# Rows left unnormalised between three attention layers, the mean taken out of the weights, and five groups of graphs in work instead of four

## The chip, the cores and the metric

The kernel runs on one core of one Trainium2 chip, in float32 throughout. The metric is device time in microseconds (us) of one execution. Before the change it takes 2701.81 us, the median of three runs (2700.86 to 2701.89). The profiled execution has a span of 2698.8 us and was itself timed at 2700.63 us; its granted TensorE clock averages 0.998. Engines are named as in the profile: PE (matmuls), DVE (VectorE), ACT (ScalarE), POOL (GpSimd), SP (the queue that issues DMAs).

## The reference

There are 128 graphs of 128 nodes, each node a row of 256 numbers `x`, and each graph has an adjacency matrix. Four layers follow one another, each adding its result to its input and normalising every row:

```python
x = layernorm(x + ggnn(x, adj, ...))          # three GRU steps, each: h@W, A^T@(...), GRU cell
x = layernorm(x + gat(x, adj, W1, a1))        # three attention layers of the form
x = layernorm(x + gat(x, adj, W2, a2))        #   Wh = x @ W.T;  e = leaky(Wh@a1 + (Wh@a2).T)
x = layernorm(x + gat(x, adj, W3, a3))        #   p = softmax(where(adj == 0, -inf, e));  p @ Wh
layernorm(x) = (x - mean(x)) / sqrt(var(x) + 1e-5)     # per row, no gain and no offset
```

In the second attention layer a node without neighbours gets zero in place of the attention result.

## The kernel before

**Groups.** Four graphs make a group (`G = 4`), so there are 32 groups. A group's rows lie as 128 partitions by 4 x 256. Each group goes through `gru` (three GRU steps) and then `gat` (three attention layers).

**GRU.** A step transposes or reads the hidden state, multiplies by the adjacency (L504), and forms the gates with a Strassen scheme: seven products of 128-row blocks per pass, two passes per step (L451, 8064 of the 14536 matmul records). DVE adds partial products (L456), ACT applies tanh (L530, L559), DVE blends (L546, L566, L569), and PE transposes the new state back (L585). The last step adds the state to `x` (L588), and the row normalisation at the end of `gru` gives `x1`.

**Attention.** Each layer of `gat` does, for its four graphs: two dot products per row against weight vectors (L611, eight DVE instructions with accumulated sums, written to `f`); PE spreads one of them over columns (L620); DVE adds the mask and takes the row maximum (L625); ACT applies the leaky slope (L629) and the exponential with its row sum (L646); PE transposes the result (L653), which is copied out of PSUM to `pT` (L655); PE multiplies the layer's input by it (L669), the product is copied out (L672), and PE multiplies by the layer's weights `gwT` (L680). DVE scales each row by the reciprocal of the softmax sum, `rden`, adds the layer's input and accumulates the row sum `total` (L686). Then comes `layernorm`.

**`layernorm` (L375 to L409).** After the GRU it uses DVE's batch statistics (L382, L384). After an attention layer it takes the mean from `total` (DVE, L391), the squares from four ACT instructions (L394), the variance plus epsilon on POOL (L397), the power -1/2 on POOL (L401), the shift on DVE (L403), and writes the normalised rows with four ACT instructions (L407). The next layer's L611 reads those rows.

**Order of the work.** Nothing is scheduled at run time. `Plan` (L48 to L195) takes the operations with assumed costs and walks a clock: an operation becomes ready when its inputs are done, and the ready one of lowest priority number starts on a free engine if buffers are free. Each engine then executes its own operations strictly in that fixed order, with waits on the others. An operation may name several engines (`EVICT` is ACT at 490 or DVE at 600), and the walk chooses. For PE, an operation whose input comes from another engine counts as ready only after that engine's `LATENCY` and a further `MARGIN` of 500 ns (L56, L117). Buffers come from pools of fixed size (L224): `gru` is a token that limits how many groups are in their GRU part (4), `k2` and `k4` hold half-size and full-size tiles, `v` small vectors. `own` (L226) reserves some of a pool for the oldest group. `stage` (L696) gives the first 28 groups their number as priority and lets the last four (`LAST = 4`) advance step by step together.

**Weights.** `score_weights` (L346) loads a layer's weights in both layouts while group 0 runs and forms the vectors `wa` that L611 uses; `gwT` is the layout that L680 reads.

Of the kernel before, what the change touches and what calls it, by code (L numbers as in the profile page):

```python
# [11 lines left out]
ALU = mybir.AluOpType  # L12
# [35 lines left out]
class Plan:  # L48
# [6 lines left out]

    MARGIN = 500  # L56

# [141 lines left out]
def adj_resnorm_kernel(  # L199
# [23 lines left out]

    pools = {"gru": 4, "xs": 2, "adj": 2, "am": 5, "k2": 26, "k4": 19, "fx": 2, "f": 3, "mv": 4, "st": 6, "v": 16,  # L224
             "gate": 5, "bank": 3}
    own = ({"k2": 8, "k4": 5, "gate": 2, "v": 5, "fx": 0, "st": 0}, {"k2": 4, "k4": 2, "v": 5, "fx": 0, "st": 0})  # L226
    floats = {"gru": 0, "k4": 1024, "xs": 1024, "fx": 256, "f": 8, "mv": 8, "st": 6, "v": 4}
    tags = {t: (n, floats.get(t, 512)) for t, n in pools.items()}
# [117 lines left out]
    def score_weights(l, prio):  # L346

        gatw, b_ = Buf("k2", KC, D), bank()
        load(gatw, gat_w[:, l], prio, start=30000)
        load(here(T(gwT)[:, l]), gat_wT[:, l], prio, start=30000)  # L350

        def fn(e):
            for h in range(2):
                for k in range(KC):
                    nc.tensor.matmul(T(b_)[:, h * D:(h + 1) * D], ga[:, l, k, h:h + 1].to_broadcast([P, P]),
                                     T(gatw)[:, k, :], start=(k == 0), stop=(k == KC - 1))
        plan.op({"PE": 4 * 432}, fn, reads=[gatw], writes=[b_], prio=prio)
        plan.op(EVICT, lambda e: copy(e, T(wa)[:, l, :, :].rearrange("p h d -> p (h d)"), T(b_)),
                reads=[b_], writes=[(wa, l)], prio=prio)
# [14 lines left out]

    def layernorm(y, total, dst, prio):  # L375

        rstd, ve, shift = Buf("v", G), Buf("v", G), Buf("v", G)
        if total is None:
            mv = Buf("mv", G, 2)
            for b in range(G):  # L380
                st = Buf("st", 6)
                plan.op({"DVE": 400}, lambda e, b=b, st=st: nc.vector.bn_stats(T(st), T(y)[:, b, :]),  # L382
                        reads=[(y, b)], writes=[st], prio=prio)
                plan.op({"DVE": 95}, lambda e, b=b, st=st: nc.vector.bn_aggr(T(mv)[:, b, :], T(st)),  # L384
                        reads=[st], writes=[(mv, b)], prio=prio)
            plan.op({"POOL": 229}, lambda e: nc.gpsimd.tensor_scalar(T(ve), T(mv)[:, :, 1], EPS, None, op0=ALU.add),
                    reads=[(mv, b) for b in range(G)], writes=[ve], prio=prio)
            less, keys = (lambda: T(mv)[:, :, 0]), [(mv, b) for b in range(G)]
        else:
            mean, ss = Buf("v", G), Buf("v", G)  # L390
            plan.op({"DVE": 100}, lambda e: nc.vector.tensor_scalar(T(mean), T(total), -1.0 / D, None, op0=ALU.mult),  # L391
                    reads=[(total, b) for b in range(G)], writes=[mean], prio=prio)
            for b in range(G):
                plan.op({"ACT": 490}, lambda e, b=b: nc.scalar.activation(  # L394
                    T(dst)[:, b, :], T(y)[:, b, :], AF.Square, bias=T(mean)[:, b:b + 1], accum_out=T(ss)[:, b:b + 1]),
                    reads=[(y, b), mean], writes=[(dst, b), (ss, b)], prio=prio)
            plan.op({"POOL": 229}, lambda e: nc.gpsimd.tensor_scalar(  # L397
                T(ve), T(ss), 1.0 / D, EPS, op0=ALU.mult, op1=ALU.add),
                reads=[(ss, b) for b in range(G)], writes=[ve], prio=prio)
            less, keys = (lambda: T(mean)), [mean]  # L400
        plan.op({"POOL": 1035}, lambda e: nc.gpsimd.tensor_tensor(T(rstd), T(ve), neghalf, ALU.pow),  # L401
                reads=[ve], writes=[rstd], prio=prio)
        plan.op({"DVE": 100}, lambda e: nc.vector.scalar_tensor_tensor(  # L403
            T(shift), less(), -1.0 if total is None else 1.0, T(rstd), op0=ALU.mult, op1=ALU.mult),
            reads=keys + [rstd], writes=[shift], prio=prio)
        for b in range(G):
            plan.op({"ACT": 500}, lambda e, b=b: nc.scalar.activation(  # L407
                T(dst)[:, b, :], T(y)[:, b, :], AF.Identity, bias=T(shift)[:, b:b + 1], scale=T(rstd)[:, b:b + 1]),
                reads=[(y, b), shift, rstd], writes=[(dst, b)], prio=prio)  # L409

    def sums(ms, prio):
# [65 lines left out]
    def gru(g, stage):  # L477
# [119 lines left out]
        x1 = Buf("k4", G, D)  # L597
        layernorm(y, None, x1, prio)
        return x1, am

    def gat(g, xc, no, stage):

        for l in range(3):
            prio = stage(g, STEPS + l)
# [3 lines left out]
            for h in (1, 0):  # L608
                for b in range(G):
                    fx = Buf("fx", D)  # L610
                    plan.op({"DVE": 345}, lambda e, b=b, h=h, l=l, f=f, fx=fx, xc=xc: nc.vector.scalar_tensor_tensor(  # L611
                        T(fx), T(xc)[:, b, :], 1.0, T(wa)[:, l, h, :], op0=ALU.mult, op1=ALU.mult,
                        accum_out=T(f)[:, b, h:h + 1]), reads=[(xc, b), (wa, l)], writes=[fx, (f, 2 * b + h)], prio=prio, port=BOTH)
            e_, pT, y = Buf("k2", G, P), Buf("k2", G, P), Buf("k4", G, D)
            top, nmax, den, rden, total = Buf("v", G), Buf("v", G), Buf("v", G), Buf("v", G), Buf("v", G)
            b_ = bank()
# [34 lines left out]
            def fn(e, b_=b_, e_=e_):  # L651
                for b in range(G):
                    nc.tensor.transpose(T(b_)[:, b * P:(b + 1) * P], T(e_)[:, b, :], ident)  # L653
            plan.op({"PE": 440}, fn, reads=[(e_, b) for b in range(G)], writes=[b_], prio=prio)
            plan.op(EVICT, lambda e, b_=b_, pT=pT: copy(e, T(pT).rearrange("p b j -> p (b j)"), T(b_)),  # L655
                    reads=[b_], writes=[pT], prio=prio)
            plan.op({"DVE": 100}, lambda e, rden=rden, den=den: nc.vector.reciprocal(T(rden), T(den)),
                    reads=[(den, b) for b in range(G)], writes=[rden], prio=prio)
            if l == 1:
                plan.op({"DVE": 100}, lambda e, rden=rden, some=some: nc.vector.tensor_mul(T(rden), T(rden), T(some)),  # L660
                        reads=[rden, some], writes=[rden], prio=prio)

            aT = []
# [10 lines left out]
            for b0 in range(0, G, 2):  # L674
# [9 lines left out]
                for b in (b0, b0 + 1):  # L684
                    plan.op({"DVE": 410}, lambda e, b_=b_, b=b, b0=b0, y=y, rden=rden, xc=xc, total=total:
                            nc.vector.scalar_tensor_tensor(  # L686
                                T(y)[:, b, :], T(b_)[:, (b - b0) * D:(b - b0 + 1) * D], T(rden)[:, b:b + 1],
                                T(xc)[:, b, :], op0=ALU.mult, op1=ALU.add, accum_out=T(total)[:, b:b + 1]),
                            reads=[b_, rden, (xc, b)], writes=[(y, b), (total, b)], prio=prio)
            xn = Buf("k4", G, D)  # L690
            layernorm(y, total, xn, prio)
            xc = xn
        plan.op({"SP": 60}, lambda e: nc.sync.dma_start(out[g * G:(g + 1) * G].rearrange("b n d -> n b d"), T(xc)),
# [56 lines left out]
```

## Time and profile before

| | before |
|---|---|
| timed runs, median (lowest to highest) | 2701.81 us (2700.86 to 2701.89) |
| span of the profiled execution | 2698.8 us |
| busy: PE / DVE / ACT / POOL | 2655.6 / 2019.6 / 1758.2 / 603.7 us |
| instructions: PE / DVE / ACT / POOL | 14536 / 6195 / 4633 / 749 |
| L611 dot products, DVE, x768 | 290.3 us |
| L407 normalised rows, ACT, x512 | 263.6 us |
| L394 squares, ACT, x384 | 190.2 us |
| L686 scale and add, DVE, x384 | 169.9 us |
| L403 shift and L391 mean, DVE | 35.0 and 25.4 us |
| HBM traffic | 62.7 MB, 23 GB/s |

The page gives the busy time of each engine, its share of the span, and the same in 40 equal slices as tenths. A group's row gives the line, engine, tiles, shapes and count, then its total and mean duration, then the idle time of that engine ahead of it and what ended that idle time. A busy PE is not the same as a PE at its rate, since the ends of matmuls are modelled; the distance between starts in the timeline is the better measure. All DMA queues together use under a tenth of the DMA engines' time.

### The profile page before, as it was taken

Reading aid. Unit: us, or ns where it says so; the run is one execution under the profiler, and the core shown is the slowest. Engines: PE = TensorE matmul, PEld = TensorE weight load, DVE = VectorE, ACT = ScalarE, POOL = GpSimd, SP = SyncE. Lnnn points to the kernel's source line nnn. Section 1 sums busy time; section 2 is a strip of 40 time slices with the busy share of each in tenths; the row PEclk is TensorE's granted clock in tenths of the full one; section 3 lists DMA queues with packets and bytes.
Section 4 is the critical chain, followed back from the end, with each engine's and each line's share of the span. In section 5 each row is a group of like instructions: output and inputs, shape, how many; then the busy total and the mean of one; then the engine's idle time right before and its main releaser. Section 6 shows DMA issues by size and latency. Waiting matters only on the chain.

```text
span 2698.8 us, 42460 instructions
## 1 busy us (share of the span) xinstructions
PE 2655.6 (98%) x14536; PEld 2366.9 (88%) x14536; DVE 2019.6 (75%) x6195; ACT 1758.2 (65%) x4633; POOL 603.7 (22%) x749
## 2 busy tenths in 40 slices
PE   8999999999999999999999999999999999999997
PEld 7888889898888888888888888988988988888875
DVE  4676777787777787778777777877778776786796
ACT  4565667666667576666666676666666676765478
POOL 1123222222121221222221221211222211322111
PEclk9999999999999999999999999999999999999999
DMA  3100000000000000001010000000000100000000
GB/s 106 32 13 28 28 13 24 28 29 20 16 21 20 28 28 28 28 1 36 21 36 13 20 24 21 28 28 20 17 28 21 36 21 1 24 9 22 19 1 32
DMA packets 70105, 65.39 MB, mean 24 GB/s; under 512 B 2688, under 2 KB 68224, under 8 KB 69888
## 3 DMA queue, kind: packets, MB, share of 16 engines
q1 hardware_dynamic: 69456, 62.66, 7.7%
q8 instruction: 114, 1.87, 0.3%
q14 instruction: 103, 0.84, 0.1%
q10 hardware_dynamic: 432, 0.01, 0.0%
HBM read 45.89 MB, written 16.78 MB: 23 GB/s over the span
## 4 chain that ended last, share of the span: by engine, by line
PE 90%; DVE 6%; ACT 2%; issue 1%; DMA 0%; POOL 0%; POOLq 0%; ACTq 0%; SPq 0%; DVEq 0%
PE gate L451 61%; PE bank L680 10%; PE bank L504 6%; PE bank L669 6%; PE bank L585 3%; PE bank L620 1%; PE bank L653 1%; DVE fx L611 1%; PE bank L369 1%; PE bank L338 1%; DVE k L686 1%; ACT k L407 1%; DVE k L456 1%; DVE k L289 1%; ACT k L394 0%
## 5 line engine op out<-in xcount | busy, mean ns | idle before, releaser
L451 PE MATMUL gate<-k,whs 128*128 128x256 f32 x4032 | 1201.6, 380 | 3.0 <-DVE k L456 1.4
L451 PE MATMUL gate<-k,wcs 128*128 128x256 f32 x4032 | 1199.2, 379 | 0.0
L451 PEld LDWEIGHTS gate<-k,wcs 128*128 128x128 f32 x4032 | 766.1, 190 | 104.0
L451 PEld LDWEIGHTS gate<-k,whs 128*128 128x128 f32 x4032 | 728.5, 190 | 85.3 <-DVE k L456 2.7
L456 DVE TENSOR_TENSOR k<-gate,k 128x512 f32<-128x512 f32 x576 | 390.4, 686 | 242.3 <-PE gate L451 200.2
L287 ACT COPY k<-bank 128x512 f32<-128x512 f32 (+1 forms) x456 | 262.2, 583 | 207.4 <-PE bank L669 60.9
L680 PE MATMUL bank<-gwT,k 128*128 128x256 f32 x1536 | 350.4, 380 | 3.3 <-ACT k L287 1.5
L680 PEld LDWEIGHTS bank<-gwT,k 128*128 128x128 f32 x1536 | 289.7, 190 | 46.0 <-DVE k L289 4.3
L611 DVE SCALAR_TENSOR_TENSOR fx<-k,wa 128x256 f32<-128x256 f32 x768 | 290.3, 436 | 40.3 <-ACT k L407 38.2
L421 POOL TENSOR_TENSOR k<-k,k 128x256 f32<-128x256 f32 x288 | 236.0, 838 | 372.8 <-DVE k L569 103.6
L394 ACT ACTIVATE k<-k,v 128x256 f32<-128x256 f32 x384 | 190.2, 497 | 185.6 <-DVE v L391 185.1
L407 ACT ACTIVATE k<-k,v,v 128x256 f32<-128x256 f32 x512 | 263.6, 591 | 55.9 <-DVE v L403 53.9
L530 ACT ACTIVATE k<-k,brz 128x512 f32<-128x512 f32 (+1 forms) x384 | 226.9, 620 | 93.2 <-DVE k L456 93.1
L686 DVE SCALAR_TENSOR_TENSOR k<-bank,v,k 128x256 f32<-128x256 f32 x384 | 169.9, 480 | 147.0 <-PE bank L680 145.8
L512 ACT COPY k<-gate 128x512 f32<-128x512 f32 x288 | 164.6, 579 | 127.9 <-PE gate L451 127.0
L564 POOL TENSOR_TENSOR k<-k,k 128x512 f32<-128x512 f32 x82 | 108.5, 1324 | 418.0 <-ACT k L559 418.0
L669 PEld LDWEIGHTS bank<-k,k 128*128 128x128 f32 x1536 | 187.1, 193 | 14.6 <-ACT k L287 5.4
L669 PE MATMUL bank<-k,k 128*128 128x128 f32 x1536 | 189.8, 277 | 8.0 <-DVE k L289 4.0
L289 DVE COPY k<-bank 128x512 f32<-128x512 f32 x228 | 154.3, 684 | 56.2 <-PE bank L504 18.3
L559 ACT ACTIVATE k<-k,bi 128x512 f32<-128x512 f32 x192 | 136.8, 720 | 76.3 <-DVE k L556 59.2
L397 POOL TENSOR_SCALAR v<-v 128x4 f32<-128x4 f32 x96 | 21.1, 220 | 739.3 <-ACT k L394 733.3
L421 POOL TENSOR_TENSOR k<-k 128x256 f32<-128x256 f32 x117 | 100.2, 858 | 340.4 <-DVE k L569 118.2
(78 smaller groups left out, 3166.8 us busy)
## 6 DMA issues: line engine op xcount, KB each, us to landing
xs<-in_x_dram SPq DMA_DIRECT2D x32, 512.0 KB, 3.9
k<-in_x_dram SPq DMA_DIRECT2D x32, 512.0 KB, 3.9
out_dram<-k SPq DMA_DIRECT2D x32, 512.0 KB, 2.9
adj<-in_adj_dram SPq DMA_DIRECT2D x32, 256.0 KB, 2.8
k<-in_gnn_wT_dram SPq DMA_DIRECT2D x3, 256.0 KB, 4.8
k<-in_w_ihT_dram SPq DMA_DIRECT2D x2, 384.0 KB, 5.7
k<-in_w_hhT_dram SPq DMA_DIRECT2D x2, 384.0 KB, 5.7
k<-in_gat_w_dram SPq DMA_DIRECT2D x3, 256.0 KB, 5.1
```

The lines of the kernel that those rows point to most:

```text
L287: nc.scalar.copy(dst, src)
L289: nc.vector.tensor_copy(dst, src)
L394: plan.op({"ACT": 490}, lambda e, b=b: nc.scalar.activation(T(dst)[:, b, :], T(y)[:, b, :], AF.Square, bias=T(mean)[:, b:b + 1], accum_out ...
L407: plan.op({"ACT": 500}, lambda e, b=b: nc.scalar.activation(T(dst)[:, b, :], T(y)[:, b, :], AF.Identity, bias=T(shift)[:, b:b + 1], scale= ...
L421: nc.vector if e == "DVE" else nc.gpsimd).tensor_tensor(T(t)[:, j, :], a(), b(), ALU.subtract),
L451: nc.tensor.matmul(T(dst)[:, j * H:(j + 1) * H], T(w)[:, m, gt, :], moving(m, ms)[1](), start=first and n == 0, stop=n == len(todo) - 1, s ...
L456: plan.op({"DVE": 630}, lambda e: nc.vector.tensor_add(T(o)[:, :, j * H:(j + 1) * H], T(b_).rearrange("p (g n) -> p g n", g=2), T(part).re ...
L530: nc.scalar.activation(T(o)[:, gt, n0:n1], src(), AF.Tanh, bias=brz[:, gt * KC + c:gt * KC + c + 1], scale=0.5)
L611: plan.op({"DVE": 345}, lambda e, b=b, h=h, l=l, f=f, fx=fx, xc=xc: nc.vector.scalar_tensor_tensor(T(fx), T(xc)[:, b, :], 1.0, T(wa)[:, l, ...
L669: nc.tensor.matmul(T(b_)[:, b * P:(b + 1) * P], T(xc)[:, b, c * P:(c + 1) * P], T(pT)[:, b, :], start=True, stop=True)
L680: nc.tensor.matmul(T(b_)[:, (b - b0) * D:(b - b0 + 1) * D], T(aT[k])[:, b * P:(b + 1) * P], T(gwT)[:, l, k, :], start=(k == 0), stop=(k == ...
L686: nc.vector.scalar_tensor_tensor(T(y)[:, b, :], T(b_)[:, (b - b0) * D:(b - b0 + 1) * D], T(rden)[:, b:b + 1], T(xc)[:, b, :], op0=ALU.mult ...
```

## The change

Five things change together.

1. Before use, each row of `gwT` (one input feature, 256 outputs) has its mean over the outputs subtracted: six times batch statistics, aggregation and a subtraction on DVE, once per kernel. The attention result added to a row then has mean zero, and a row whose input has mean zero keeps it, so the mean need not be taken again after a layer.
2. After an attention layer the rows are not scaled. `y` itself is the next layer's input. `deviation` computes what the variance needs (four ACT squares into a scratch tile `jx`, without a bias), and `power` the factor per row, `rstd`. The epsilon is scaled along with the row: with `before` from the previous layer, two small DVE instructions replace the POOL one.
3. In layers 2 and 3 the factor enters where it is needed: the dot products `f` are multiplied by `rstd` (two DVE instructions of 128x4), `pT` is scaled while it leaves PSUM (one DVE instruction of 128x512, or four ACT instructions of 128x128), and `rden` is multiplied by the previous variance and factor (two DVE instructions of 128x4), which returns the result to the unscaled rows' size.
4. After the third layer four ACT instructions scale the rows in place before the output's DMA. L686 (L728 after) loses its accumulated row sum.
5. The planner gets other numbers: `MARGIN` 300 instead of 500, five `gru` tokens instead of four, `k4` 18 instead of 19, a pool `jx`, more of `f` and `v`, other reservations, and adjusted assumed costs of the batch statistics and of L686.

```diff
-    MARGIN = 500
+    MARGIN = 300
...
-    pools = {"gru": 4, "xs": 2, "adj": 2, "am": 5, "k2": 26, "k4": 19, "fx": 2, "f": 3, "mv": 4, "st": 6, "v": 16,
+    pools = {"gru": 5, "xs": 2, "adj": 2, "am": 5, "k2": 26, "k4": 18, "fx": 2, "jx": 2, "f": 4, "mv": 4, "st": 6, "v": 24,
              "gate": 5, "bank": 3}
-    own = ({"k2": 8, "k4": 5, "gate": 2, "v": 5, "fx": 0, "st": 0}, {"k2": 4, "k4": 2, "v": 5, "fx": 0, "st": 0})
+    own = ({"k2": 12, "k4": 5, "gate": 2, "v": 5, "fx": 0, "jx": 0, "st": 0}, {"k2": 4, "k4": 3, "v": 5, "fx": 0, "jx": 0, "st": 0})
...
+        for k in range(KC):
+            st, mv = Buf("st", 6), Buf("mv", G, 2)
+            plan.op({"DVE": 330}, lambda e, k=k, st=st: nc.vector.bn_stats(T(st), T(gwT)[:, l, k, :]), ...)
+            plan.op({"DVE": 110}, lambda e, st=st, mv=mv: nc.vector.bn_aggr(T(mv)[:, 0, :], T(st)), ...)
+            plan.op({"DVE": 330}, lambda e, k=k, mv=mv: nc.vector.tensor_scalar(
+                T(gwT)[:, l, k, :], T(gwT)[:, l, k, :], T(mv)[:, 0, 0:1], None, op0=ALU.subtract), ...)
...
+    def deviation(y, before, prio):
+        ss, ve = Buf("v", G), Buf("v", G)
+        for b in range(G):
+            jx = Buf("jx", D)
+            plan.op({"ACT": 490}, lambda e, b=b, jx=jx: nc.scalar.activation(
+                T(jx), T(y)[:, b, :], AF.Square, accum_out=T(ss)[:, b:b + 1]), ...)
+        if before is None:
+            plan.op({"POOL": 229}, lambda e: nc.gpsimd.tensor_scalar(
+                T(ve), T(ss), 1.0 / D, EPS, op0=ALU.mult, op1=ALU.add), ...)
+        else:
+            eps = Buf("v", G)
+            plan.op({"DVE": 100}, lambda e: nc.vector.tensor_scalar(T(eps), T(before), EPS, None, op0=ALU.mult), ...)
+            plan.op({"DVE": 100}, lambda e: nc.vector.scalar_tensor_tensor(
+                T(ve), T(ss), 1.0 / D, T(eps), op0=ALU.mult, op1=ALU.add), ...)
+        return ve
...
+                if l:
+                    plan.op({"DVE": 100}, lambda e, h=h, f=f, rstd=rstd: nc.vector.tensor_mul(
+                        T(f)[:, :, h], T(f)[:, :, h], T(rstd)), ...)
...
+            if l:
+                def scaled(e, b_=b_, pT=pT, rstd=rstd):
+                    if e == "DVE":
+                        nc.vector.tensor_mul(T(pT), T(b_).rearrange("p (b j) -> p b j", b=G),
+                                             T(rstd).unsqueeze(2).to_broadcast([P, G, P]))
+                    else:
+                        for b in range(G):
+                            nc.scalar.mul(T(pT)[:, b, :], T(b_)[:, b * P:(b + 1) * P], T(rstd)[:, b:b + 1])
+                plan.op({"DVE": 630, "ACT": 1100}, scaled, reads=[b_, rstd], writes=[pT], prio=prio)
...
+            if l:
+                for by in (ve, rstd):
+                    plan.op({"DVE": 100}, lambda e, rden=rden, by=by: nc.vector.tensor_mul(T(rden), T(rden), T(by)), ...)
...
-                                T(xc)[:, b, :], op0=ALU.mult, op1=ALU.add, accum_out=T(total)[:, b:b + 1]),
+                                T(xc)[:, b, :], op0=ALU.mult, op1=ALU.add),
...
-            xn = Buf("k4", G, D)
-            layernorm(y, total, xn, prio)
-            xc = xn
+            xc, ve = y, deviation(y, ve, prio)
+            rstd = power(ve, prio)
+        for b in range(G):
+            plan.op({"ACT": 500}, lambda e, b=b: nc.scalar.mul(T(xc)[:, b, :], T(xc)[:, b, :], T(rstd)[:, b:b + 1]), ...)
```

## The prediction

> **What bounds the kernel now.** I read the page first, then distances between matmul starts in PE's timeline, then the table of stretches, then groups and waits, and last the chain at the end.
>
> ```profile
> PE 2655.6 (98%) x14536; PEld 2366.9 (88%) x14536; DVE 2019.6 (75%) x6195; ACT 1758.2 (65%) x4633; POOL 603.7 (22%) x749
> PE   8999999999999999999999999999999999999997
> DVE  4676777787777787778777777877778776786796
> ACT  4565667666667576666666676666666676765478
> ```
>
> PE is the only engine near full, in every slice but the first and the last. In the last slices DVE reaches 9 and ACT 8 while PE falls to 7: another regime.
>
> ```profile
> 165.47 0.59 PE L451 MATMUL gate<-k,wcs 128*128 128x256 f32 x2
> 165.90 0.60 PE L620 MATMUL bank<-ident,f 128*128 128x128 f32 x4
> 166.34 0.60 PE L451 MATMUL gate<-k,whs 128*128 128x256 f32 x2
> ...
> 2592.48 0.59 PE L451 MATMUL gate<-k,wcs 128*128 128x256 f32 x2
> ...
> 2683.99 4.07 PE L680 MATMUL bank<-gwT,k 128*128 128x256 f32 x16
> ```
>
> Starts give PE's real rate: two 256-wide matmuls take 0.43 us (0.216 each), four transposes 0.44 (0.11 each); an L669 or L504 matmul takes 0.112 (13 of them in 1.45 us from 149.77). By the counts of the groups: (8064 + 1536) x 0.216 = 2073.6; (1536 + 1536) x 0.112 = 344; 1792 transposes x 0.109 = 195; the weights' products (L338, L355) about 21. Sum 2634 us. The change leaves every matmul, so this is the floor. The other 65 us of 2698.8: 5.0 ahead of the first matmul, 10.8 after the last one ends (2688.06), and 49 of waits between. The tail: after the last gate matmul (ends about 2592.9) the order has 69.3 us of PE work left, done in 95.2 us, so 25.9 us are waits. That leaves 23 for the rest.
>
> ```profile
> 50.00:150.00 100.00, 95.30 (x513) 84.28 (x512) 63.72 (x136) 49.15 (x109) 16.99 (x18) 1.00 0.08 24
> 150.00:600.00 450.00, 448.43 (x2473) 401.55 (x2472) 338.13 (x1015) 291.84 (x766) 106.32 (x132) 1.00 0.08 23
> 1800.00:2400.00 600.00, 597.57 (x3314) 536.20 (x3313) 460.49 (x1409) 403.64 (x1064) 148.00 (x186) 1.00 0.07 22
> 2600.00:2620.00 20.00, 15.11 (x72) 11.97 (x73) 19.21 (x108) 17.28 (x57) 4.47 (x8) 0.91 0.00 1
> 2640.00:2660.00 20.00, 14.62 (x86) 11.71 (x84) 18.65 (x114) 19.00 (x66) 2.40 (x4) 1.00 0.01 2
> 2680.00:2699.00 19.00, 6.25 (x35) 4.81 (x33) 4.13 (x19) 10.78 (x30) 2.40 (x4) 0.85 0.25 83
> ```
>
> Columns after the length: PE, PEld, DVE, ACT, POOL busy, clock, DMA. The middle has no room (PE 99.6%, DVE 75 to 77%). In the ramp (50 to 150) PE idles 4.7 us. In the tail DVE is at 96% and later ACT at 95%. I put the 23 us at 12 up to 150 us and 11 in the 2400 us after; the table shows only part of these, since it counts modelled matmul ends as busy.
>
> ```profile
> L407 ACT ACTIVATE k<-k,v,v 128x256 f32<-128x256 f32 x512 | 263.6, 591 | 55.9 <-DVE v L403 53.9 <-DVE mv L384 1.6
> L403 DVE SCALAR_TENSOR_TENSOR v<-v,v 128x4 f32<-128x4 f32 x96 | 29.3, 305 | 59.8 <-POOL v L401 59.4
> L660 DVE TENSOR_TENSOR v<-v,v 128x4 f32<-128x4 f32 x32 | 6.0, 188 | 0.7
> ```
>
> The normalisation is long as a chain, but its waits are ACT's and DVE's. In the middle PE has other groups to work on meanwhile.
>
> ```profile
> 2632.88 0.88 ACT k L646 x4
> 2633.76 1.97 ACT k L407 x4
> 2635.73 1.97 ACT k L394 x8
> ```
>
> In the tail this chain (start, length, what) is the end-setting path, and here ACT's normalising stands on it.
>
> **The Trainium skill.** (1) "Perfetto Trace Analysis", Identifying the Most-Contended Engine: matmul busy share is no good measure, as pipelined matmuls overlap. The trace agrees: a gate matmul is recorded at 380 ns while starts are 216 apart; hence my floor. (2) The same page, Optimization Strategy: a kernel can have regimes with different most-contended engines. It does here, see the stretches. (3) "VectorE: DVE Perf Modes", Rules for kernel authors: fewer instructions matter more than fewer semaphores. The trace agrees: a 128x4 multiply is recorded at 188 ns for four elements. (4) "ScalarE: Activation LUTs", Step-by-step: what each stage is for: a per-row scale is part of the instruction. The trace agrees: L407, with scale and bias, starts every 0.49 us, the squares every 0.495.
>
> **The change part by part, whole kernel.** Counts are those of the two instruction orders, durations busy time per instruction.
>
> ACT: 384 normalisations x 0.515 = -198; final scaling 128 x 0.515 = +66; 55 fewer copies x 0.575 = -32; 132 scaled 128x128 evictions. These are new: bounded by L629 (0.32, same shape) and L519 (0.366, PSUM source, twice as wide); I take 0.34, +45. Sum -119, ACT 1639 us. The squares stay.
>
> DVE, removed: mean 25.4, shift 29.3, accumulator reads of L686 384 x 0.083 = 31.7, nine copies 6, eight subtractions L564 6: -98. Added: two f multiplies and two rden multiplies in 64 layers, 256 x 0.188 = 48; scaled epsilon 64 x 0.264 and variance 64 x 0.237 = 32; 31 scaled pT evictions, bounded by the copy (0.68) and L564 (0.735), 0.68 taken, 21; 75 L421 subtractions that the planner moves from POOL, 31; weights' mean 6 x 0.81 = 5. +137. Sum +39, DVE 2059 us, 76% of the span. L686 without its sum could also be shorter (L553 0.41 against 0.44): up to -12. Either way PE hides it in the middle.
>
> POOL: 64 variance instructions (14) and 75 L421 (62) fewer, eight L564 (11) more: -65. DMAs are the same; the output's waits for L735 as it did for L407.
>
> Latency of one layer change: before, L391 0.2, squares 2.1, POOL 0.3 and 1.1, L403 0.2, normalising 2.1, last dot products 0.4: 6.4 us. After, the eight dot products (2.8) run beside squares 2.1, variance 0.2, power 1.1, f multiply 0.2: 3.6. So 2.8 shorter, twice per group. New wait: the f multiply (L639) waits for POOL's power, and behind it on DVE stand the next group's masks and adds, for which PE waits. It replaces L403's wait on the same instruction (59.4 us in all), so I cost it at no change.
>
> **What that does to the 65 us.** *Start and end*, 15.8: same, since the last layer still ends with squares, power, scaling and the DMA.
>
> *Ramp*, 12: the fifth group gives PE work, while the weights' mean adds 4 to 5 us to a DVE that is 64% busy. Between -5 and +5; I take -1.
>
> *Middle*, 11: more groups and a less loaded ACT help; MARGIN places PE operations 0.2 us earlier after their input and hurts. Between -8 and +24 (below); I take -2.
>
> *Tail*, 25.9: after the last gate the new order holds 73.2 us of PE work, 3.9 more, so gates end sooner. The last GRU transpose is followed by 68.1 against 62.5 us of PE work. In start-to-start steps (L611 0.345, L625 0.21, L686 0.405 before and about 0.33 after, copies 0.61, small ones about 0.1), DVE after its last GRU blend has 72 us before and 72 after; ACT after its last tanh has 82 before and 74 after (36 normalisations fewer). DVE was held for 92 us (2600.6 to 2692.9) with these 72. With DVE's load unchanged only ACT's 8 us and 2 x 2.8 of latency can come back. The drain from the last L620 (2669.4) to the end, 29.4, stays, as the same 14.5 us of PE work follow it in both. Ahead of it I expect DVE as full as in its best stretch: 62 us at 95%, 65 instead of 69: -4. Of the 5.6 us of PE work moved behind the last transpose, about 3 are a gain, as a gate's result needs 8.8 us to that transpose and fewer matmuls now fill it (4.7 instead of 6.8). Sum -7; bounds -18 (PE alone limits up to the drain) and +6 (waits as before, small DVE operations at their full 0.19).
>
> Sum: -1 - 2 - 7 = -10: 2698.8 becomes 2688.8. The median of the timed runs lies 3.0 over that span, so 2692.
>
> **Rivals.** *A, margin turns into waits (slower).* A group has 74 PE operations, 32 groups 2368. Each may now stand 0.2 us sooner: at most 474 us, at least nothing. If one in twenty arrives late by all of it, 118 x 0.2 = 24 us: 2716. It decides when the middle's waits grow by over 15 us, one operation in 31. For: DVE's queue is in order, and POOL's L421 is recorded at 838 ns against 720 assumed. Against: PE in the middle loses under half a per cent with many groups ready, and DVE and ACT steps lie within a few per cent of the planner's costs. *B, tail bound by DVE as before (no change).* DVE's 72 us are the same, its small instructions more; 2700. For: 96% in 2600 to 2620. Against: the chain there runs on ACT from 2632 to 2640. *C, the tail nearly closes.* Waits fall to ramp 8, middle 7, tail 8, end 10.5: 2634 + 5 + 33.5 = 2672.5, so 2676. For: ACT 10% lighter there. Against: DVE. That the change does not do what it says is excluded by the counts: 384 normalisations are gone.
>
> **How the numbers follow.** Forecast 0.50 (2684 to 2697), A 0.15, B 0.20, C 0.15. 0.2%, about what can be told from no change, is 5.4 us. Faster: 0.47 of the forecast, C and 0.02 of B, 0.64. Same: 0.18 of B, 0.02 of the forecast, 0.20. Slower: A and the forecast's rest, 0.16. 2680 to 2709 leaves out most of C (0.11) and the larger part of A (0.09).
>
> **What would show it.** Right: ACT near 1640 and DVE near 2060 us; the middle stretches still at 99.6% PE; in the last 100 us fewer idle us of PE, and no normalising in the chain between layers. Wrong: PE waits on DVE sums or ACT copies in the middle (A); DVE full from 2600 to 2690 and the end where it was (B); a ramp that loses over 15 us behind the weights' statistics.

## The result, and the profile after

The changed kernel takes 2684.76 us, the median of six runs (2683.13 to 2685.58); run beside it, the kernel before takes 2701.85 us (2700.52 to 2703.69). The ratio is 0.9937, with a 95% interval of 0.9924 to 0.995: 17.1 us, or 0.6%, faster. The profiled execution was timed at 2684.54 us and has a span of 2682.8 us, 16.0 less than before.

From the page of the kernel after, the busy times and the slices of three engines:

```profile
PE 2650.4 (99%) x14536; PEld 2367.5 (88%) x14536; DVE 2069.0 (77%) x6111; ACT 1611.6 (60%) x4453; POOL 549.7 (20%) x618
PE   8999999999999999999999999999999999999988
DVE  5677677887777877778877778777878777786787
ACT  4555666565656666566556566656666665655467
```

The matmuls are the same 14536, so the floor is the same 2634 us, and the 16 us came out of PE's waits. ACT lost 146.6 us of work and DVE gained 49.4, and neither figure explains 16 us. The last slices of PE read 8 and 8 where they read 9 and 7. Now the stretches of the kernel after (columns after the length: PE, PEld, DVE, ACT, POOL busy, clock, DMA share, GB/s):

```profile
50.00:150.00 100.00, 96.88 (x536) 86.21 (x535) 66.30 (x149) 51.72 (x114) 21.27 (x23) 1.00 0.10 27
800.00:1400.00 600.00, 600.00 (x3320) 539.23 (x3319) 473.73 (x1396) 364.67 (x1007) 125.24 (x141) 1.00 0.08 23
1400.00:2000.00 600.00, 600.00 (x3330) 539.51 (x3330) 474.99 (x1429) 366.72 (x1018) 126.22 (x142) 1.00 0.08 23
2600.00:2620.00 20.00, 16.82 (x92) 13.82 (x91) 19.03 (x113) 15.91 (x66) 2.82 (x4) 0.91 0.00 0
2640.00:2660.00 20.00, 19.59 (x124) 17.69 (x123) 19.55 (x113) 17.12 (x71) 3.15 (x3) 1.00 0.01 2
```

The two middle stretches are the striking lines: PE is busy 600.00 of 600.00 us, twice. The same two before:

```profile
800.00:1400.00 600.00, 597.91 (x3293) 535.89 (x3292) 461.69 (x1419) 397.46 (x1052) 141.76 (x174) 1.00 0.08 23
1400.00:2000.00 600.00, 599.69 (x3329) 539.15 (x3328) 457.92 (x1416) 396.94 (x1047) 138.78 (x175) 1.00 0.08 25
```

In the tail DVE is at least as full as it was (95 and 98%, before 96 and 93%), ACT is no longer (80 and 86% where it was 86 and 95%), and PE gets 19.59 of 20 us from 2640 where it got 14.62.

To put the gain in its places I used the measure of the prediction on every kernel: the distance between consecutive matmul starts, less the step of that line (0.216, 0.112 or 0.109 us), summed by stretch. "End" is from the last matmul's start to the end of the span; "tail" is from the last gate matmul on. The middle is 150 us to the last gate matmul.

| waits of PE, us | to 150 | 150-800 | 800-1400 | 1400-2000 | 2000 to last gate | middle, sum | tail | end | span |
|---|---|---|---|---|---|---|---|---|---|
| before | 11.8 | 3.3 | 3.6 | 0.6 | 3.6 | 11 | 25.5 | 11.1 | 2698.8 |
| after | 10.2 | 3.8 | -0.3 | -0.4 | 1.2 | 4 | 21.0 | 8.8 | 2682.8 |

So the 16 us are 1.6 of the ramp, 6.8 of the middle, 4.5 of the tail and 2.3 of the end; the last 0.8 lies among the weights' products, for which this measure has no exact step. (Values of -0.3 and -0.4 are its rounding: no waits at all.)

### The profile page after: what moved, and what is told of

Its sections match the earlier page's. It is cut to its first block, busy times and chain, and to the rows that moved or that the text cites. A ratio compares the mean times of both kernels' runs of the same rounds, so it can differ in the third digit from the quotient of the medians.

```text
span 2682.8 us, 41895 instructions
## 1 busy us (share of the span) xinstructions
PE 2650.4 (99%) x14536; PEld 2367.5 (88%) x14536; DVE 2069.0 (77%) x6111; ACT 1611.6 (60%) x4453; POOL 549.7 (20%) x618
## 4 chain that ended last, share of the span: by engine, by line
PE 93%; DVE 4%; ACT 1%; issue 1%; DMA 0%; POOL 0%; POOLq 0%; SPq 0%; ACTq 0%; DVEq 0%
PE gate L473 63%; PE bank L722 11%; PE bank L526 6%; PE bank L711 6%; PE bank L607 3%; PE bank L681 1%; PE bank L648 1%; DVE fx L635 1%; PE bank L380 1%; PE bank L338 1%; DVE k L728 1%; DVE k L289 0%; DVE k L568 0%; DVE k L478 0%; DVE k L653 0%
## 5 line engine op out<-in xcount | busy, mean ns | idle before, releaser
L478 DVE TENSOR_TENSOR k<-gate,k 128x512 f32<-128x512 f32 x576 | 389.3, 684 | 207.9 <-PE gate L473 184.0
L287 ACT COPY k<-bank 128x512 f32<-128x512 f32 (+1 forms) x401 | 229.5, 584 | 206.8 <-PE bank L607 91.3
L389 POOL TENSOR_TENSOR v<-v,neghalf 128x4 f32<-128x4 f32 x128 | 134.4, 1050 | 857.7 <-DVE v L428 840.3
L635 DVE SCALAR_TENSOR_TENSOR fx<-k,wa 128x256 f32<-128x256 f32 x768 | 285.9, 426 | 24.3 <-ACT k L408 24.2
L417 ACT ACTIVATE jx<-k 128x256 f32<-128x256 f32 x384 | 156.5, 408 | 231.0 <-DVE k L728 230.7
L443 POOL TENSOR_TENSOR k<-k,k 128x256 f32<-128x256 f32 x229 | 175.9, 789 | 450.0 <-DVE k L289 223.2
L728 DVE SCALAR_TENSOR_TENSOR k<-bank,v,k 128x256 f32<-128x256 f32 x384 | 167.2, 476 | 106.8 <-PE bank L722 106.6
L289 DVE COPY k<-bank 128x512 f32<-128x512 f32 x219 | 150.1, 686 | 114.0 <-PE bank L711 88.6
L586 POOL TENSOR_TENSOR k<-k,k 128x512 f32<-128x512 f32 x90 | 133.3, 1492 | 303.4 <-ACT k L581 284.2
L588 DVE SCALAR_TENSOR_TENSOR k<-k,k 128x512 f32<-128x512 f32 x192 | 170.1, 886 | 2.2 <-POOL k L586 1.1
L674 ACT ACTIVATE k<-k,v 128x128 f32<-128x128 f32 x384 | 148.9, 389 | 30.8 <-DVE v L670 30.2
```

Source lines behind the costliest of these rows:

```text
L287: nc.scalar.copy(dst, src)
L443: nc.vector if e == "DVE" else nc.gpsimd).tensor_tensor(T(t)[:, j, :], a(), b(), ALU.subtract),
L478: plan.op({"DVE": 630}, lambda e: nc.vector.tensor_add(T(o)[:, :, j * H:(j + 1) * H], T(b_).rearrange("p (g n) -> p g n", g=2), T(part).re ...
L588: plan.op({"DVE": 620}, lambda e, d=d, o=o: nc.vector.scalar_tensor_tensor(T(d), T(o)[:, 1, :], 1.0, T(d), op0=ALU.add, op1=ALU.mult), rea ...
L728: nc.vector.scalar_tensor_tensor(T(y)[:, b, :], T(b_)[:, (b - b0) * D:(b - b0 + 1) * D], T(rden)[:, b:b + 1], T(xc)[:, b, :], op0=ALU.mult ...
```

## The experiments

Two theories stood at the start: W, that the lighter arithmetic (no normalising between the layers) brought the gain, and G, that the planner's new numbers (five groups, the smaller margin, the reservations) did. The experiments first took each part alone.

### The arithmetic alone, and parts of the planner's numbers undone

`e1_algebra_only` is the kernel after with the old margin, groups and reservations; its pool sizes and assumed costs stay:

```diff
-    MARGIN = 300
+    MARGIN = 500
-    pools = {"gru": 5, ...
+    pools = {"gru": 4, ...
-    own = ({"k2": 12, "k4": 5, ...}, {"k2": 4, "k4": 3, ...})
+    own = ({"k2": 8, "k4": 5, ...}, {"k2": 4, "k4": 2, ...})
```

> The changed kernel with the planner's old numbers: MARGIN 500, four gru tokens, the old reservations (the larger pools of f and v and k4 18 stay, since the new operations need them). Theory W (the work itself: ACT lighter by 146 us and a shorter change between layers) expects most of the gain: 2686 to 2691, waits of PE in the middle (150 to 2550 us) at 6 us or less, the tail as short as in the changed kernel. Theory G (five groups and the planner's numbers) expects under half of the gain: 2693 to 2699, with the middle's waits near 11 us as before and a shorter tail only. I lean to W.

Measured: 2716.41 us (2716.14 to 2716.73), ratio 1.0055 (1.0038 to 1.0072): slower than before, which neither W nor G had allowed for. The arithmetic alone does not bring the gain, so W falls; that it loses is a second question.

`e3_after_margin500` is the kernel after with only the margin put back:

```diff
-    MARGIN = 300
+    MARGIN = 500
```

> The changed kernel with MARGIN 500 alone put back. If the lower margin turned into waits (the prediction's rival A), this is faster than the changed kernel, 2676 to 2681. If the margin is without effect, it is within 3 us of 2685. If the lower margin is part of the gain (PE operations are not held back in the planner's walk when they could run), it is 2688 to 2693. I expect the middle case.

Measured: 2698.88 us, ratio 0.9991 (0.9982 to 1.0). That is more than any of the three cases allowed. The smaller margin is worth 14 us here, with the opposite sign to what rival A feared from it.

`e4_after_gru4` is the kernel after with four groups in work:

```diff
-    pools = {"gru": 5, ...
+    pools = {"gru": 4, ...
```

> The changed kernel with four gru tokens instead of five. If the fifth group is what emptied the middle's waits, they come back to 8 to 11 us and the time is 2690 to 2696, and the ramp up to 150 us loses 2 to 3 us more. If it is the lighter ACT, the middle stays under 5 us and the time is within 3 us of 2685. I lean to the second, with some loss in the ramp.

Measured: 2724.43 us, ratio 1.0084 (1.0069 to 1.0099). One token less costs 40 us, where 11 at most were expected. Read alone, that would make the fifth group the cause of everything.

### The planner's numbers alone

`e2b_planner_only` is the kernel before, its arithmetic untouched, with the new margin, five groups and the new reservations (the pools `f` and `v` grow by one tile each); `e7_before_gru5` has only the fifth group. The first form of it, `e2_planner_only`, had `v` at 24 as in the kernel after and gave no time: with `k4` still at 19 its tiles need 153.19 KB per partition where 153.09 are left.

```diff
-    MARGIN = 500
+    MARGIN = 300
-    pools = {"gru": 4, ... "f": 3, ... "v": 16, ...
+    pools = {"gru": 5, ... "f": 4, ... "v": 17, ...
-    own = ({"k2": 8, "k4": 5, ...}, {"k2": 4, "k4": 2, ...})
+    own = ({"k2": 12, "k4": 5, ...}, {"k2": 4, "k4": 3, ...})
```

> The kernel before with the changed kernel's planner numbers alone: MARGIN 300, five gru tokens, the new reservations, f 4 and v 17; rows are normalised as before. Theory P (the fifth group, with the numbers around it, is what empties the middle; the new arithmetic alone cost 15 us with the old numbers) expects 2684 to 2692, most or all of the gain. Theory I (it needs both: ACT lighter and five groups) expects 2696 to 2705. Theory L (each set of numbers draws another fixed order, and how well that order fits the real durations decides, not any one number) expects anything from 2690 to 2715, with the waits of PE in a few clumps in the middle. I lean to L over I over P.

> The kernel before with five gru tokens and nothing else. P expects 2688 to 2696 with a shorter ramp and fewer waits in the middle. I expects 2697 to 2704. L expects a move of 5 us or more either way, 2692 to 2715.

Measured: 2728.12 us, ratio 1.0103 (1.0086 to 1.012), above what any of the three theories allowed, and 2708.00 us, ratio 1.0027 (1.0016 to 1.0037), which only theory L allows. The arithmetic alone is 0.55% slower, the planner's numbers alone are 1.03% slower, and both together are 0.63% faster. No sum of two separate effects gives that, so G falls as well; and the fifth group, which saved 40 us against e4, costs 0.27%, some 7 us, here. Something else is decided by these numbers.

### Twenty nanoseconds of margin

`e5_after_margin320` and `e5b_after_margin280` are the kernel after with the margin 20 ns up and down. A margin that matters as a margin would change the time a little.

```diff
-    MARGIN = 300
+    MARGIN = 320      (and 280)
```

> The changed kernel with MARGIN 320 instead of 300, a change that no mechanism prices at more than 1 us, and that gives another order on PE from the first few hundred instructions on. L expects it to move by 5 us or more, most likely up, to 2690 to 2705, because the middle of the changed kernel (about 4 us of waits in 2400) can hardly be improved by chance. P and I expect 2685 within 4 us.

> The changed kernel with MARGIN 280, the other side. As for 320: L expects a move of 5 us or more, 2690 to 2705; P and I expect 2685 within 4 us.

Measured: 2684.23 us, ratio 0.994 (0.9925 to 0.9955), as the kernel after; and 2714.28 us, ratio 1.0049 (1.0034 to 1.0064), 30 us above it. The expectation from L, a move of 5 us or more, came true on one side only, and there beyond its 2690 to 2705. So the margin acts through the fixed order that it makes (with the walk's choice of engines, which comes with it), not through its size. What distinguishes the good orders can be seen in PE's timeline of the kernel after, one stretch and the stretch 81.61 us later:

```profile
1001.52 0.60 PE L607 MATMUL bank<-ident,k 128*128 128x128 f32 x4
...
1006.35 1.95 PE L711 MATMUL bank<-k,k 128*128 128x128 f32 x16
...
1083.13 0.60 PE L607 MATMUL bank<-ident,k 128*128 128x128 f32 x4
...
1087.96 1.95 PE L711 MATMUL bank<-k,k 128*128 128x128 f32 x16
```

Both pairs are 81.61 us apart, which is the floor of one group (32 groups in 2634 us, less the 21 us of weights' products, are 81.66 each). The order has become periodic: after one group's worth of PE instructions it repeats itself. I compared PE's fixed order with itself one group later, instruction by instruction, in the middle part (30 to 70% of it). In the kernel after and in e5 every instruction agrees. In the kernel before, e1, e2b, e3, e4, e5b and e7 only 38 to 52% do. e5b in the same stretch, and one of its waits, from its stretches, its chain and PE's timeline:

```profile
800.00:1400.00 600.00, 592.52 (x3245) 527.21 (x3244) 465.67 (x1338) 354.69 (x970) 133.47 (x151) 1.00 0.08 23
```

```profile
1672.08 0.68 DVE f L639
...
1674.92 0.58 DVE v L663
...
1675.97 1.66 ACT k L674 x8
```

```profile
1676.52 1.48 PE L681 MATMUL bank<-ident,k 128*128 128x128 f32 x4 [1.26 <-ACT k L674]
```

PE stands 1.26 us for the exponential of one group, behind a chain in which two small instructions of 128x4 took 0.68 and 0.58 us instead of 0.16. The first, L639, is one of the added multiplications; the second, L663, is in the kernel before too (L635). When they take so long comes below.

### Is it the repetition? Two orders chosen for it

Theory R: a repeating order is what removes the waits of the middle, with either arithmetic and any number of groups. Its rival: five groups or the lighter ACT do. Following the planner's walk for other values of its numbers shows which of them fall into a repeating order. With four groups the new arithmetic does so at a margin of 360, and the old arithmetic at 410, there from about 30% of the kernel on.

```diff
 e9, against after            e8, against before
-    MARGIN = 300             -    MARGIN = 500
+    MARGIN = 360             +    MARGIN = 410
-    pools = {"gru": 5, ...
+    pools = {"gru": 4, ...
```

> The changed kernel with four gru tokens and MARGIN 360. With four tokens and MARGIN 300 it took 2724 us; this pair gives a repeating order again, from a tenth of the kernel on. R expects 2680 to 2690 and next to no waits in the middle. Theory F (the fifth group is needed for the changed kernel to run well) expects 2705 or more.

> The kernel before with MARGIN 410 alone: old arithmetic, four gru tokens. Its fixed order on PE repeats exactly from group to group from about a third of the kernel on, as the orders of the changed kernel and of its MARGIN 320 variant do, and as those of all other kernels tried so far do not. Theory R (the middle's waits vanish where the order repeats with one group's period, whatever the arithmetic and the tokens) expects under 1 us of waits in each 600 us after 800 us, and a time of 2688 to 2696: before's 2701.5 less most of its 11 us in the middle, with the tail as long as before (25 us or more). Theory A (the repeating order helps only with the lighter ACT) expects 4 us or more of waits in each 600 us and 2697 to 2710.

Measured: e9 2692.02 us, ratio 0.9967 (0.9955 to 0.9978), 32 us below the other kernel with four groups (e4), so five groups are not needed. One stretch of e4 and then of e9:

```profile
800.00:1400.00 600.00, 593.15 (x3252) 529.61 (x3251) 471.43 (x1349) 356.87 (x987) 129.90 (x147) 1.00 0.08 23
800.00:1400.00 600.00, 600.00 (x3320) 539.23 (x3319) 473.95 (x1397) 364.15 (x1008) 125.45 (x142) 1.00 0.08 24
```

e8 2703.17 us, ratio 1.0007 (1.0 to 1.0014): no gain. In both the waits between 800 and 2000 are what R expected, but the times lie above its ranges, e9 by 2 us and e8 by 7. The stretches of e8 tell why:

```profile
800.00:1400.00 600.00, 600.00 (x3320) 539.69 (x3319) 450.45 (x1433) 400.07 (x1061) 127.07 (x156) 1.00 0.08 25
...
2000.00:2400.00 400.00, 394.54 (x2177) 353.29 (x2176) 306.87 (x967) 267.44 (x712) 86.52 (x105) 0.99 0.07 20
```

With the old arithmetic and ACT at 400 us of 600, PE again waits for nothing where the order repeats. On the way into the pattern (150 to 800) and out of it (after 2000) this order loses 11.9 and 10.6 us where the kernel before loses 3.3 and 3.6, more than the 5 us that it saves between 800 and 2000. The table, sorted by whether the middle repeats:

| waits of PE, us | repeats | to 150 | 150-800 | 800-1400 | 1400-2000 | 2000 to last gate | tail | end |
|---|---|---|---|---|---|---|---|---|
| after | yes | 10.2 | 3.8 | -0.3 | -0.4 | 1.2 | 21.0 | 8.8 |
| e5 (after, margin 320) | yes | 10.6 | 2.9 | -0.3 | -0.4 | 0.0 | 22.6 | 8.8 |
| e9 (after, four groups, 360) | yes | 9.7 | 6.3 | -0.3 | -0.4 | 2.5 | 24.8 | 8.7 |
| e8 (before, margin 410) | yes | 6.7 | 11.9 | -0.4 | -0.4 | 10.6 | 25.1 | 11.5 |
| before | no | 11.8 | 3.3 | 3.6 | 0.6 | 3.6 | 25.5 | 11.1 |
| e7 (before, five groups) | no | 9.4 | 9.4 | 4.3 | 3.7 | 3.7 | 25.9 | 11.1 |
| e2b (planner's numbers alone) | no | 9.8 | 8.8 | 5.6 | 5.1 | 7.3 | 39.7 | 11.2 |
| e3 (after, margin 500) | no | 8.0 | 1.4 | 11.7 | 1.8 | 8.2 | 19.7 | 8.8 |
| e5b (after, margin 280) | no | 8.6 | 7.5 | 13.0 | 11.0 | 1.5 | 22.7 | 8.8 |
| e1 (arithmetic alone) | no | 10.3 | 7.5 | 9.4 | 8.9 | 11.6 | 19.9 | 8.8 |
| e4 (after, four groups) | no | 12.2 | 10.3 | 12.9 | 9.5 | 10.9 | 19.2 | 8.8 |

Two readings. The stretches from 800 to 2000 depend on the order: no waits where it repeats, whichever arithmetic. The end depends on the arithmetic: 8.7 to 8.8 with the new and 11.1 to 11.5 with the old in every order. The tail is 19.2 to 24.8 with the new and 25.1 to 39.7 with the old, but the order moves it within one arithmetic by more than the gap between them (24.8 in e9, 25.1 in e8).

One rival of R stays open. The walk that makes an order has waits of its own: run again from each kernel's text, it gives the order of PE that the trace shows, and with its assumed costs PE stands idle between 800 and 2000 for 0 to 4.6 us in the orders that repeat and for 5.7 to 16.5 in those that do not. So repetition and the absence of waits may both come from a walk that keeps PE fed; that the one causes the other is not shown.

### Where the order does not repeat: the small DVE instructions

In orders that do not repeat, the middle loses 11, 21 and 27 us with the old arithmetic and 23, 33, 37 and 44 with the new. Two theories: S, that the added small multiplications on DVE (L639, L702) cost it, being held up while POOL works; O, that the waits belong to these orders, whatever the small instructions cost. `e12_gru4_without_small` keeps the order of e4 instruction by instruction and leaves out only the 256 multiplications of 128x4, so that the scores and the attention result are not scaled:

```diff
-                    plan.op({"DVE": 100}, lambda e, ...: nc.vector.tensor_mul(T(f)[:, :, h], T(f)[:, :, h], T(rstd)), ...)
+                    plan.op({"DVE": 100}, lambda e: None, ...)
...
-                    plan.op({"DVE": 100}, lambda e, ...: nc.vector.tensor_mul(T(rden), T(rden), T(by)), ...)
+                    plan.op({"DVE": 100}, lambda e: None, ...)
```

> The changed kernel with four gru tokens (2724 us, 44 us of PE waits between 150 us and the last gate) in exactly its fixed order, but without the 256 small multiplies of 128x4 that the new arithmetic adds on DVE (f by rstd and rden by two factors): they keep their places in the planner's walk and issue nothing, so the scaling of the scores and of the attention result is left out. In the trace of the kernel with them they are recorded at 267 and 281 ns where their median is 160, because they are held while POOL works. Theory S (these small instructions on DVE, with their waits for POOL, make the clumps of PE waits in the middle) expects 2695 to 2712 and under 25 us of middle waits. Theory O (the clumps belong to the order itself: PE's queue stands at operations whose inputs come late, whatever DVE's small ones cost) expects 2717 to 2724 and 38 us or more. I lean to O.

Measured: 2711.78 us (2710.05 to 2712.18), ratio 1.0038 (1.0024 to 1.0051), 12.6 us less than e4. The time is in the range of S, but by the measure of the table the middle of e12 still loses 6.0, 11.1, 6.3 and 9.3 us: 33 where e4 lost 44, S expected under 25 and O 38 or more. So the multiplications cost this order 11 us in the middle, and most of the waits stay without them. e12 takes away three things at once: the instructions, their being held up, and the wait of L639 for POOL's power. The other 33 us were in no run separated further. The planner's walk, with its own costs, has 20 us of waits in this stretch of the same order; whether they are the same waits was not followed. With the old arithmetic the walk's waits between 800 and 2000 (5.7, 8.3 and 10.2 us) are close to those measured (4.2, 8.0 and 10.7); with the new, PE waits 13.5, 24.0 and 22.4 us in e3, e5b and e4 where the walk has 7.2, 16.2 and 10.0, and 18.3 in e1 where it has 16.5. The groups of e4 and then of the kernel after, for these instructions:

```profile
L702 DVE TENSOR_TENSOR v<-v,v 128x4 f32<-128x4 f32 x128 | 36.0, 281 | 3.0
L639 DVE TENSOR_TENSOR f<-f,v 128x4 f32<-128x4 f32 x128 | 31.2, 268 | 15.8 <-POOL v L389 15.6
```

```profile
L639 DVE TENSOR_TENSOR f<-f,v 128x4 f32<-128x4 f32 x128 | 16.6, 164 | 24.5 <-POOL v L389 24.3
L702 DVE TENSOR_TENSOR v<-v,v 128x4 f32<-128x4 f32 x128 | 23.3, 182 | 3.0
```

The same instruction has a mean of 268 or 164 ns. Split by whether POOL was busy when it started: in e4 L639 takes 157 ns with POOL idle (87 times) and 503 with POOL busy (41 times, up to 1227). Being held is not enough to cost time, though: in e5, which has no waits there, L639 has a mean of 255 ns.

### The tail: three and six groups at the end

`LAST` says how many groups advance together at the end. With a margin of 340, whose middle repeats too, I tried three and six instead of four.

```diff
-    MARGIN = 300
+    MARGIN = 340
-    LAST = 4
+    LAST = 3          (and 6)
```

> The changed kernel with MARGIN 340 and three instead of four groups that advance together at the end. Its order repeats in the middle. If the tail's waits (21 us with four) come from DVE being full with four groups in the same stage, three have less work left behind the last gate product, and the time falls to 2672 to 2682. If they come from the chain of one group's three layers, fewer groups hide it worse: 2686 to 2700. I lean to the second.

> The changed kernel with MARGIN 340 and six groups that advance together at the end, the other side. If the tail is bound by DVE's work behind the last gate product, more groups in the same stage put more attention work there: 2690 to 2710. If the chain of one group is what it waits for, six hide it better: 2675 to 2683.

Measured: 2703.25 us, ratio 1.0007 (1.0 to 1.0013), and 2733.13 us, ratio 1.0118 (1.0103 to 1.0133), both above every range that was expected of them, so neither theory of the tail is borne out by the two together. The margin of 340 with four groups was not run. With three, the tail holds only 55.1 us of PE work and waits 30.5 us, and 9.7 more come before the last gate. With six, 31.0 us of waits come before the last gate and 38.9 after it. Why three loses before the last gate too was not followed further. Four stays the best of the three, and no kernel here beats the one after by more than its runs differ (e5: 2684.23).

## Why the prediction came out as it did

**The sum was near, and in part by luck.** 2684.76 us lies at the edge of the forecast's 2684 to 2697. The prediction's steps against what the runs show:

| step | predicted | measured |
|---|---|---|
| start and end | 0 | -2.3 (all at the end) |
| ramp | -1 | -1.6 |
| middle | -2 | -6.8 |
| tail | -7 | -4.5 |
| sum of the span | -10 | -16.0 (0.8 unplaced) |

The ramp's -1.6 is within what the orders differ by (6.7 to 12.2 in the table of all kernels), and was not followed.

**Middle: the mis-sized term, and for a wrong reason.** I gave it -2 because "more groups and a less loaded ACT help", with the smaller margin against it. The sign holds; the reason does not. e9 empties the middle with four groups and e8 with the old ACT load, while e1 and e4 have the light ACT and lose 37 and 44 us. What emptied the middle is the order that the planner's walk makes with this set of numbers, one that repeats, as that of before does not. That is a draw, and the forecast was lucky in it: at 280 instead of 300 the same change is 0.49%, or 13 us, slower than before, and at 500 it is within 0.2% of it. Why a repeating order has no waits was not tried by itself. A possible reason, beside the walk's own waits: a relation between two groups that is good once is good in every period, while a wandering order passes through bad ones.

**Rival A** (the margin turns into waits, 24 us) named a real risk in the wrong place. e5b has 33 us of waits in the middle, about what A foresaw, but with a margin only 20 ns smaller, and e3 with 500 loses 23. No price per operation of the margin fits these three.

**Tail: right in kind, -4.5 instead of -7.** DVE was said to set it with its load unchanged, and ACT's load to be what can come back. The stretches show that (DVE 95 to 99% from 2600 to 2660, ACT 68 to 86%), and the chain between the layers runs on DVE where it ran on ACT's normalising. That DVE sets the tail is read from these views; e10 and e11 do not bear it out. From the chain of the kernel after:

```profile
2646.96 0.88 DVE fx L635 x5
...
2649.69 0.79 DVE k L728 x2
...
2651.54 3.72 PE bank L722 x16
```

Two terms go the way of the difference, and are together more than its 2.5 us; what each took was not separated. I put L686 at a step of 0.33 us after the change, because its row sum is gone; L728 in fact starts every 0.398 us, where L686 started every 0.409 (medians of back-to-back pairs). The 31.7 us of accumulator reads did vanish from the groups, but a read lies beside the next instruction, so dropping it frees 0.011 us each. 48 of them in the tail at 0.068 are 3.3 us of DVE more than in my sum. The second is a long wait right behind the last gate matmul, from the timelines of PE and ACT after:

```profile
2579.34 0.59 PE L473 MATMUL gate<-k,wcs 128*128 128x256 f32 x2
2583.56 1.63 PE L681 MATMUL bank<-ident,k 128*128 128x128 f32 x4 [3.62 <-ACT k L674]
```

```profile
2578.91 2.08 ACT L408 ACTIVATE k<-k,v,v 128x256 f32<-128x256 f32 x4 [2.89 <-issue]
```

ACT stood 2.89 us at L408, the normalising behind the last group's GRU, until the statistics on DVE (from 2575.14), POOL's power (to 2578.41) and the shift (L404, 2578.67) were done, with another group's leaky slope and exponentials (L657, L674) queued behind it. I had followed what stands behind a waiting instruction on DVE (L639), and not on ACT.

**End: nought predicted, -2.3 measured, in every kernel with the new arithmetic.** I had written that the drain of 29.4 us behind the last L620 stays. After the change it is 25.4 (2657.37 to 2682.8). From ACT's timeline, before and then after:

```profile
2689.24 0.51 ACT L394 ACTIVATE k<-k,v 128x256 f32<-128x256 f32 x1 [1.53 <-DVE v L391]
...
2692.97 2.07 ACT L407 ACTIVATE k<-k,v,v 128x256 f32<-128x256 f32 x4 [1.66 <-DVE v L403]
```

```profile
2675.48 0.40 ACT L417 ACTIVATE jx<-k 128x256 f32<-128x256 f32 x1
2677.28 1.70 ACT L735 ACTIVATE k<-k,v 128x256 f32<-128x256 f32 x4 [1.31 <-POOL v L389]
```

Before, the four squares waited for the mean of all four graphs (L391) and were done 3.25 us after the last matmul ended at 2688.06 (1.66 us ahead of L407's start). After, they start in pairs as L728 finishes, and are done 1.6 us after the last matmul's end at 2674.37 (1.31 us ahead of L735's start): -1.65. The hop from squares to scaling went from 1.66 to 1.31 us, the scaling from 2.07 to 1.70. My list of what the change removes had the mean as an instruction of 25.4 us of DVE in all, but not as the wait that it is.

**Loads.** ACT fell by 146.6, not 119. I had written that the squares stay. They do, but without a bias each is shorter; the kernel after, and then before:

```profile
L417 ACT ACTIVATE jx<-k 128x256 f32<-128x256 f32 x384 | 156.5, 408 | 231.0 <-DVE k L728 230.7 <-DVE fx L635 0.2
L735 ACT ACTIVATE k<-k,v 128x256 f32<-128x256 f32 x128 | 54.3, 498 | 3.5 <-POOL v L389 3.3
```

```profile
L394 ACT ACTIVATE k<-k,v 128x256 f32<-128x256 f32 x384 | 190.2, 497 | 185.6 <-DVE v L391 185.1
```

408 ns with no per-row operand, 497 or 498 with one, and 591 (L407) with two: 89 to 94 ns for each. The Trainium skill, "ScalarE: Activation LUTs", under What ACT_TABLE_LOAD costs, states 93 ns for each pointer operand; the traces agree. I had read of the same page only that a scale is part of the instruction, and took that for no cost. DVE rose by 49.4 instead of 39. The largest excess stands where DVE and POOL meet: L588, the same blend as L566 before, went up by 29.9 us (before, then after), with POOL busy at its start 54 times where it was 29; the two kinds of added multiplications took 39.9 us instead of the 48 that I gave them.

```profile
L566 DVE SCALAR_TENSOR_TENSOR k<-k,k 128x512 f32<-128x512 f32 x192 | 140.2, 732 | 6.4 <-POOL k L564 5.7
L588 DVE SCALAR_TENSOR_TENSOR k<-k,k 128x512 f32<-128x512 f32 x192 | 170.1, 886 | 2.2 <-POOL k L586 1.1
```

**The new wait at L639**, costed at no change, is in the groups with 24.3 us behind POOL's power, less than the 59.4 that stood at L403. That step held. **Rivals B and C**: DVE is full in the tail as B said, yet the tail is 4.5 us shorter and the end 2.3; C's tail of 8 us was never near (19.2 at best in the table).

## What to carry to other kernels

In a kernel whose engines run a fixed order, compare a change over several orders that differ in nothing that matters (here 20 ns of a planner's margin): one order may be worth more than the change, 30 us here, against the 3 to 9 us by which tail and end together are shorter with the new arithmetic in every order of the table than in the kernel before. Look first for a periodic order, and for one in which the planner's own walk leaves the busiest engine few gaps; then keep the ways into and out of it short, since e8 lost more there than it won. When a value is no longer needed, count the wait for it as well as the instruction, and take the price of an instruction from starts, as the read of an accumulator hardly costs anything there.

## What the runs showed of the hardware

**DVE held while POOL works.** Of the kernel after, the blend L588 takes 682 ns when POOL is idle at its start (138 times) and 1407 when POOL is busy (54 times); L568 684 and 1112; the multiplication L702 162 and 242, up to 1198. Instructions with an input from PSUM show no such difference: L478 takes 687 and 679 ns, the copy L289 687 and 678. The Trainium skill, "SBUF — State Buffer", Who interferes with whom, says that only the port pair shared by VectorE and GpSimd contends, as an exclusive lock; the traces agree in what is slowed and what is not, and no run here shows the lock itself. What I had not expected is that an instruction of four elements per row, on which a whole group's chain hangs, can so become as long as one of 512, and that leaving out 256 of them, with their waits, is worth 12.6 us (e12).

**A long wait need not cost PE anything.** In e5 L702 takes 523 ns on the 56 occasions when POOL is busy, more often than in the kernel after (32), and PE waits for nothing from 800 to 2000. In e5b, whose order does not repeat, held instructions stand at the head of the wait of PE shown above; how many of its waits begin so was not counted.
